# Reordering the first steps of a layernorm, attention and gated-FFN kernel

## The chip, the core and the metric

The kernel runs on one core of a Trainium2 chip. The core has five engines that each work through their own instructions in order: TensorE (PE in the profile: matmuls and transposes through the matrix array; PEld is its weight loads), VectorE (DVE), ScalarE (ACT), GpSimd (POOL) and SyncE (SP, which here only issues DMAs). They meet through semaphores. The metric is device time in microseconds (us), from start to end of the program. Lower is better.

## The reference, cut to what matters

Input x is 4 batches of 512 rows with 512 elements, in float32. All of it is computed:

```python
xn = layernorm(x)                                  # over the 512 elements, eps 1e-5
q = einsum("bpd,hde->bphe", xn, W_Q) + b_Q         # 16 heads of 128; k and v alike
s = where(causal, einsum("bqhe,bkhe->bhqk", q, k) / sqrt(128), -1e5)
z = einsum("bkhe,bhqk->bqhe", v, softmax(s))
attn = einsum("bqhe,hed->bqd", z, W_O) + b_O
f = (silu(xn @ gate_w.T * gate_s) * (xn @ up_w.T * up_s)) @ down_w.T * down_s
out = x + attn * silu(f)
```

The FFN's inner width is 1408. Its weights are -1, 0 or 1.

## The kernel before, in words

**Split numbers.** Matmuls run in a reduced float32 format. To keep precision, each operand is held as two parts: "hi" is the value rounded to that format (a cast, mostly on ScalarE), "lo" is what is left (a subtraction, on VectorE or GpSimd). A product is three matmuls: hi·hi, lo·hi and hi·lo. Two helpers issue them. `mm3` (lines 91 to 94) does one pair of operands in the order hi·lo, hi·hi, lo·hi. `mm3_all` (96 to 106) does a list of pairs: all hi·hi, then all lo·hi, then all hi·lo, and after each matmul it takes one step from the list `side`, if there is any. So steps put into `side` are woven between the matmuls of a projection.

**Order of work.** The whole program lies in a manual schedule: every engine runs its instructions in the order in which the Python code issues them. Nothing is planned by costs. Moving a line in the code moves its instructions in the queues of the engines that it uses.

**Buffers.** PSUM, where matmuls write, has two pools of tiles here: `ps_st` with three buffers (scores, even transposes) and `ps_mm` with five (projections `psq`, `psk`, `psv`, attention output `z`, output projection `pso`, odd transposes). A buffer can be written again when all readers of its former tile are done; for most tiles the last reader is the "lo" subtraction on VectorE.

**The start** (lines 517 to 569). Tiles of 128 rows of x are loaded. `ln_stats` does two VectorE instructions for each tile (statistics, aggregate), `ln_sd` a square root on ScalarE (which needs an activation table load), `ln_normalize` a reciprocal and a scaling on VectorE (tile `xn`). `ln_transpose` does four TensorE transposes per tile and the cast to hi on ScalarE (tile `xh`); `ln_low` is the lo part on VectorE (`xl`). Weights are loaded raw by `prepare`, which puts them on the list `pending` with a due number, and are split when `split_pending` is called with that number: a cast on ScalarE (line 150) and a subtraction (151) on GpSimd, or on the engine that is given. The first head's q and k are projected in halves, between the transposes of tiles 0, 1 and 2, 3.

**The heads** (581 to 681). 64 heads follow each other: eight groups of two attention heads, in each group four batches, in each batch two heads. The step of number n does, in this order: scores and softmax of head n (`softmax`: three score tiles on TensorE, four fused maximum steps on VectorE, four exponentials on ScalarE, four reciprocals on VectorE with a layernorm step of the list `between` after each if there is one, four scalings on GpSimd, line 342); for early heads the split of the former head's transposed p (`split_p`: cast at line 389 on ScalarE, subtraction at line 391 on VectorE, for early heads both halves there); the first projections of v (`fill`); the 32x32 transposes of p on VectorE (`turn_p`, 356), whose blocks a DMA round trip puts in place; weight splits that are due (`split_pending(n)`, line 617); loads; q and k projections of the next head; attention output z of the former head (`attend`, 423); and the rest of the v projections.

In steps 0, 2 and 4 (`ln_next`) the next batch's x is normalised too. Its statistics come a step before (`ln_b`, 644 and 658); in step 0 all four tiles come right before the projection of q. Its four `ln_normalize` steps stand in the list `norms`: in step 0 they run after q's projection (650), in steps 2 and 4 inside softmax. Its 16 transposes and four lows go into `side` and are woven into the last two v projections (662 to 668).

The output weights of group 0 (`wo0`, two tiles) are prepared in step 1 with due number 2, and first used by `pso` in step 3. The FFN (691 to 798) follows after all heads.

Of the kernel before, what the change touches and what calls it, by code (L numbers as in the profile page):

```python
# [43 lines left out]
def kernel(  # L44
# [46 lines left out]
    def mm3(ps, a, b, first, last):  # L91
        nc.tensor.matmul(ps, a.hi, b.lo, start=first, stop=False)  # L92
        nc.tensor.matmul(ps, a.hi, b.hi, start=False, stop=False)  # L93
        nc.tensor.matmul(ps, a.lo, b.hi, start=False, stop=last)  # L94

    def mm3_all(ps, pairs):

        todo = [
            (getattr(a, i), getattr(b, k))
            for i, k in (("hi", "hi"), ("lo", "hi"), ("hi", "lo"))  # L100
            for a, b in pairs
        ]
        for n, (l, r) in enumerate(todo):
            nc.tensor.matmul(ps, l, r, start=n == 0, stop=n == len(todo) - 1)  # L104
            if side:
                side.pop(0)()
# [5 lines left out]
    with ExitStack() as at:  # L112
# [15 lines left out]
        def load_x(b, t):  # L128
            xt = lnp.tile([P, D], F32, name="xt", tag="xt")
            nc.sync.dma_start(out=xt, in_=x[b, ts(t, P), :])  # L130
            x_in[b, t] = xt
# [5 lines left out]
        def load_const(src, shape, name):  # L137
            t = const.tile(shape, F32, name=name)
            nc.gpsimd.dma_start(out=t, in_=src)
            return t  # L140
# [5 lines left out]
            load_on[0].dma_start(out=r, in_=src)  # L146
            return r

        def split_w(dst, raw, on=nc.gpsimd):
            nc.scalar.copy(dst.hi, raw)  # L150
            on.tensor_tensor(dst.lo, raw, dst.hi32, ALU.subtract)

        def flat(s):
            return Split(s.hi.rearrange("p c e -> p (c e)"), s.lo.rearrange("p c e -> p (c e)"))
# [10 lines left out]

        def split_pending(n, on=nc.gpsimd):

            for due, dst, raw in [p for p in pending if p[0] <= n]:
                split_w(dst, raw, on)
            pending[:] = [p for p in pending if p[0] > n]  # L170

        def prepare(due, dst, src, name):

# [21 lines left out]

        mv_of, ln_of = {}, {}

        def ln_stats(b, tt):

            mv = small.tile([P, len(tt), 2], F32, name="mv")  # L200
            for k, t in enumerate(tt):
                st = small.tile([P, 6], F32, name="st")
                nc.vector.bn_stats(out=st, in_=x_in[b, t])
                nc.vector.bn_aggr(out=mv[:, k, :], in_=st)
            mv_of[b, tuple(tt)] = mv

        def ln_sd(b, tt):
            mv = mv_of.pop((b, tuple(tt)))
            sd = small.tile([P, len(tt)], F32, name="sd")
            nc.scalar.activation(sd, mv[:, :, 1], AF.Sqrt, bias=eps)  # L210
            for k, t in enumerate(tt):
                ln_of[b, t] = mv[:, k, :], sd[:, k : k + 1]
# [43 lines left out]
        def ln_low(b, t):  # L256
            lo_of.pop((b, t))()
# [38 lines left out]
        def softmax(qT, kT, between):  # L296
            p = pp.tile([P, NS * P], F32, name="p", tag="p")
            of = [p[:, row[t] : row[t] + (t + 1) * P] for t in range(NT)]
            nmax = {}
            for pack in PACK:  # L300
                sc = ps_st.tile([P, S], F32, name="sc", tag="st")
                at_ = 0
                where = {}
                for t in pack:
                    n = (t + 1) * P
                    where[t] = sc[:, at_ : at_ + n]
                    if t > 0:
                        mm3(where[t], qT[:, ts(t, P)], kT[:, :n], True, True)
                    at_ += n
                if 0 in pack:  # L310

                    two = sc[:, at_ - P : at_ + P]
                    nc.tensor.matmul(two, qT.hi[:, :P], kT.both[:, :, :P], start=True, stop=False)  # L313
                    nc.tensor.matmul(where[0], qT.lo[:, :P], kT.hi[:, :P], start=False, stop=True)
                for t in pack:
                    n = (t + 1) * P
                    add = mask[:, S - n :]
                    if t == 0:
                        add = small.tile([P, P], F32, name="add", bufs=1)
                        nc.vector.tensor_tensor(add, two[:, P:], mask[:, S - P :], ALU.add)  # L320
                    nmax[t] = small.tile([P, 1], F32, name="nmax", bufs=8)
                    nc.vector.tensor_tensor_reduce(  # L322
                        out=of[t],
                        in0=where[t],
                        in1=add,
                        scale=-SCALE,
                        scalar=BIG,
                        op0=ALU.add,
                        op1=ALU.min,
                        accum_out=nmax[t],  # L330
                    )
            for pack in PACK:
                for t in pack:
                    tot = small.tile([P, 1], F32, name="tot", bufs=8)
                    rtot = small.tile([P, 1], F32, name="rtot", bufs=8)
                    nc.scalar.activation(  # L336
                        of[t], of[t], AF.Exp, bias=nmax[t], scale=-1.0, accum_out=tot
                    )
                    nc.vector.reciprocal(rtot, tot)  # L339
                    if between:  # L340
                        between.pop(0)()
                    nc.gpsimd.tensor_scalar(of[t], of[t], rtot, 1.0, ALU.mult, ALU.mult)  # L342
            return of
# [34 lines left out]
        def split_p(raw, shared):  # L378
            pt = p_split()
            half = NQ // 2  # L380
            for k in range(0, NQ, half):
                src = raw[:, k : k + half].rearrange("p b (s i) -> p b s i", i=Q)

                def dst(part):
                    return part[:, :, k * Q : (k + half) * Q].rearrange(
                        "p s (b i) -> p b s i", i=Q
                    )

                nc.scalar.copy(dst(pt.hi), src)  # L389
                on = nc.gpsimd if shared and k == 0 else nc.vector  # L390
                on.tensor_tensor(dst(pt.lo), src, dst(pt.hi32), ALU.subtract)  # L391
            return pt
# [104 lines left out]
        def look():  # L497
            if looking:
                raw = looking.pop(0)
                nc.vector.tensor_tensor(bits, bits, raw.bitcast(I32), ALU.bitwise_or)  # L500
# [16 lines left out]
        with tc.manual_schedule():  # L517
# [22 lines left out]
            ln_transpose(0, 0)  # L540
            ln_transpose(0, 1)
            split_pending(-3)
            ln_stats(0, [2, 3])
            ln_low(0, 0)
            ln_low(0, 1)
            ln_sd(0, [2, 3])
            table(AF.Exp)
            ln_normalize(0, 2)
            ln_normalize(0, 3)
            split_pending(-2, nc.vector)  # L550
            prepare_qk(1, -1)
            q_of = project(0, 0, wq[0], bq_sb, "q", 2)
            k_of = project(0, 0, wk[0], bk_sb, "k", 2)
# [11 lines left out]
            split_pending(-1)  # L565
            for t in range(NT):
                load_x(1, t)
            bo_bc = load_const(b_o.broadcast_to([P, D]), [P, D], "bo_bc")
            ds_bc = load_const(down_s.broadcast_to([P, D]), [P, D], "ds_bc")

# [10 lines left out]
            for n, (g, b, i) in enumerate(heads):  # L581
# [12 lines left out]
                def fill(ks):  # L594
                    for t in ks:
                        if i == 0 and not (n == 0 and t == 0):
                            project_v(g, b, t)
                        if i == HG - 1 and prev is not None:
                            project_out(*prev, t, zs[prev])
# [7 lines left out]
                of = softmax(qT, kT, norms if n > 0 else [])  # L607
                if n > 1 and early:
                    pt = split_p(raw, B * HG < n < len(heads) - 2)
                look()  # L610
                half = NT // 2 if nxt is not None else NT - 1
                fill(range(0, half))
# [1 line left out]
                    raw_next = turn_p(of)  # L614
                if not early:
                    pt = split_p(raw, B * HG < n < len(heads) - 2)
                split_pending(n)

                if prev is not None:
                    cut = NT // 2 if n + HG < len(heads) else NT - 1  # L620
# [19 lines left out]
                if g > 0:  # L640
                    load_look()
                if nxt is not None:
                    if ln_b is not None and n != 1:
                        ln_stats(ln_b, range(NT))
                    nh = nxt[0] * HG + nxt[2]
                    *_, qT = project(nxt[1], nh, wq[nh], bq_sb, "q")
                    if n == 0:
                        ln_sd(ln_b, range(NT))
                        table(AF.Exp)
                    while norms:  # L650
                        norms.pop(0)()
# [7 lines left out]
                if ln_b is not None and n > 0:  # L659
                    ln_sd(ln_b, range(NT))  # L660
                    table(AF.Exp)
                if ln_next:
                    for t in range(NT):
                        side.extend(ln_transposes(b + 1, t))
                        side.append(lambda t=t: ln_low(b + 1, t))
                    fill(range(half, NT))
                    while side:
                        side.pop(0)()
                    if b + 2 < B:
                        for t in range(NT):  # L670
                            load_x(b + 2, t)
# [192 lines left out]
```

## Time and profile before

| | us |
|---|---|
| median of 3 runs | 1218.52 (1217.36 to 1219.19) |
| profiled execution | 1218.36 |
| its span, first to last instruction | 1217.0 |
| TensorE busy | 1199.1 |
| VectorE busy | 795.5 |
| ScalarE busy | 549.9 |
| GpSimd busy | 378.6 |
| mean granted TensorE clock | 0.997 of full |

In the lines of the profile, "L391" is line 391 of the kernel; "pt<-ptr,pt" names the tile written and the tiles read; "x2" counts instructions; brackets give the idle time of the engine just before, and what ended it. A line of waits gives the engine and line that waited, the engine and tile waited for, then the sum, the number and the longest in us. The share of busy time alone does not tell what a step costs: an engine may be late at one place and idle at another.

### The profile page before, as it was taken

How to read it: one execution, taken by the hardware profiler on the slowest of the kernel's cores; microseconds unless marked ns; L12 is line 12 of the kernel's file. 1: busy time of each engine (PE TensorE's matmuls, PEld its weight loads, DVE VectorE, ACT ScalarE, POOL GpSimd, SP SyncE). 2: the span in 40 equal slices, each digit the busy share in tenths (PEclk: the TensorE clock that was granted, in tenths of full speed). 3: DMA queues.
4: the chain of work that ended last, by engine and by line, in shares of the span. 5: the costliest groups of instructions: out<-in, count | busy, mean ns of one | idle time of the engine just before them, and what ended most of it. 6: DMA issues, size and time to landing. Idle time of an engine off the chain costs nothing.

```text
span 1217.0 us, 19221 instructions
## 1 busy us (share of the span) xinstructions
PE 1199.1 (99%) x6466; PEld 1047.4 (86%) x6466; DVE 795.5 (65%) x2149; ACT 549.9 (45%) x1272; POOL 378.6 (31%) x484
## 2 busy tenths in 40 slices
PE   7899999999999999999999999999999999999997
PEld 6788888888888888888888888888888888888886
DVE  6997767677777777776776676666667543433443
ACT  5654544454445545444544454545444332323231
POOL 3212332343234433432433252325231351202110
PEclk9999999999999999999999999999999999999999
DMA  5354456666665666666765655555555893727241
GB/s 168 111 177 156 150 174 194 200 193 196 191 208 173 194 206 213 191 199 203 210 184 173 186 182 172 186 179 173 175 166 166 270 306 87 216 79 217 77 147 38
DMA packets 117913, 215.55 MB, mean 177 GB/s; under 512 B 13232, under 2 KB 45744, under 8 KB 117808
## 3 DMA queue, kind: packets, MB, share of 16 engines
q1 hardware_dynamic: 74016, 134.51, 34.6%
q10 hardware_dynamic: 29376, 53.26, 14.4%
q0 software_dynamic: 14416, 26.48, 8.2%
q8 instruction: 53, 0.87, 0.3%
q14 instruction: 52, 0.43, 0.1%
HBM read 135.17 MB, written 79.04 MB: 176 GB/s over the span
## 4 chain that ended last, share of the span: by engine, by line
PE 96%; DVE 2%; ACT 0%; DMA 0%; issue 0%; SPq 0%; DVEq 0%; ACTq 0%
PE psv L104 15%; PE psq L104 14%; PE psk L104 14%; PE z L423 9%; PE pd L727 7%; PE pg L727 7%; PE pu L727 7%; PE pso L92 5%; PE pso L93 5%; PE pso L94 5%; PE sc L92 3%; PE sc L93 3%; PE sc L94 3%; PE sc L313 1%; PE tr L247 1%; PE z L426 1%
## 5 line engine op out<-in xcount | busy, mean ns | idle before, releaser
L342 POOL TENSOR_SCALAR p<-p,rtot 128x512 f32<-128x512 f32 (+3 forms) x256 | 148.6, 600 | 604.9 <-DVE rtot L339 580.3
L336 ACT ACTIVATE p<-p,nmax 128x512 f32<-128x512 f32 (+3 forms) x256 | 140.9, 553 | 111.6 <-DVE nmax L322 111.6
L356 DVE STREAM_TRANSPOSE sq<-p 128x256 f32<-128x256 f32 x378 | 113.2, 361 | 0.0
L279 ACT ACTIVATE q<-psq,consts 128x512 fp32r<-128x512 f32 (+1 forms) x65 | 44.4, 683 | 123.4 <-PE psq L104 50.3
L322 DVE CUSTOM_DVE_ANT_0 p<-sc,mask 128x512 f32<-128x512 f32 (+2 forms) x192 | 96.3, 551 | 1.3 <-PE sc L94 1.2
L280 DVE SCALAR_TENSOR_TENSOR k<-psk,consts,k 128x512 fp32r<-128x512 f32 (+1 forms) x65 | 48.1, 739 | 72.2 <-ACT k L279 72.2
L391 POOL TENSOR_TENSOR pt<-ptr,pt 128x640 fp32r<-128x640 f32 x53 | 83.7, 1580 | 8.8 <-ACT pt L389 8.4
L279 ACT ACTIVATE k<-psk,consts 128x512 fp32r<-128x512 f32 (+1 forms) x65 | 44.2, 680 | 90.4 <-PE psk L104 90.4
L389 ACT CAST pt<-ptr 128x640 fp32r<-128x640 f32 x126 | 85.0, 724 | 0.1
L280 DVE SCALAR_TENSOR_TENSOR q<-psq,consts,q 128x512 fp32r<-128x512 f32 (+1 forms) x65 | 47.9, 737 | 49.7 <-ACT q L279 48.1
L753 DVE SCALAR_TENSOR_TENSOR hd<-pu,consts,sg 128x512 f32<-128x512 f32 x44 | 33.0, 751 | 65.5 <-PE pu L727 61.0
L469 DVE TENSOR_TENSOR a<-pso,a 128x512 f32<-128x512 f32 x108 | 69.4, 682 | 0.3 <-issue 0.3
L391 DVE TENSOR_TENSOR pt<-ptr,pt 128x640 fp32r<-128x640 f32 x73 | 68.8, 953 | 1.1 <-ACT pt L389 1.1
L339 DVE RECIPROCAL rtot<-tot 128x1 f32<-128x1 f32 x256 | 41.6, 162 | 41.3 <-ACT p L336 35.1
L92 PE MATMUL sc<-k,q 128*128 128x512 f32 (+2 forms) x192 | 64.9, 338 | 1.1 <-DVE k L280 1.1
L93 PE MATMUL sc<-k,q 128*128 128x512 f32 (+2 forms) x192 | 64.7, 337 | 0.0
L94 PE MATMUL sc<-k,q 128*128 128x512 f32 (+2 forms) x192 | 64.7, 337 | 0.0
L423 PE MATMUL z<-pt,v_0h 128*128 128x512 f32 x128 | 50.7, 396 | 3.4 <-DVE pt L391 3.4
L336 ACT ACTIVATION_READ_ACCUMULATOR p<-p,nmax 128x1 f32 x256 | 47.7, 186 | 0.0
L423 PE MATMUL z<-pt,v_1h 128*128 128x384 f32 x128 | 44.2, 345 | 0.0
L783 ACT ACTIVATE o<-o 128x512 f32<-128x512 f32 (+1 forms) x17 | 10.3, 607 | 68.8 <-DVE o L782 68.8
L92 PEld LDWEIGHTS sc<-k,q 128*128 128x128 f32 x192 | 36.2, 188 | 5.3 <-DVE k L280 1.3
(762 smaller groups left out, 3418.3 us busy)
## 6 DMA issues: line engine op xcount, KB each, us to landing
turn<-sq SPq DMA_DIRECT2D x63, 640.0 KB, 3.4
ptr<-turn SPq DMA_DIRECT2D x252, 160.0 KB, 3.5
acc<-a SPq DMA_DIRECT2D x124, 256.0 KB, 3.3
a<-acc ACTq DMA_DIRECT2D x108, 256.0 KB, 3.0
xt<-in_x SPq DMA_DIRECT2D x16, 256.0 KB, 4.0
wor<-in_w_o ACTq DMA_DIRECT2D x16, 256.0 KB, 4.5
fa<-acc SPq DMA_DIRECT2D x16, 256.0 KB, 6.5
fx<-in_x SPq DMA_DIRECT2D x16, 256.0 KB, 6.9
```

Source lines behind the costliest of these rows:

```text
L92: nc.tensor.matmul(ps, a.hi, b.lo, start=first, stop=False)
L93: nc.tensor.matmul(ps, a.hi, b.hi, start=False, stop=False)
L94: nc.tensor.matmul(ps, a.lo, b.hi, start=False, stop=last)
L104: nc.tensor.matmul(ps, l, r, start=n == 0, stop=n == len(todo) - 1)
L280: nc.vector.scalar_tensor_tensor(q.lo[:, at_], ps, bias[:, h : h + 1], q.hi32[:, at_], ALU.add, ALU.subtract)
L322: nc.vector.tensor_tensor_reduce(out=of[t], in0=where[t], in1=add, scale=-SCALE, scalar=BIG, op0=ALU.add, op1=ALU.min, accum_out=nmax[t],)
L336: nc.scalar.activation(of[t], of[t], AF.Exp, bias=nmax[t], scale=-1.0, accum_out=tot)
L342: nc.gpsimd.tensor_scalar(of[t], of[t], rtot, 1.0, ALU.mult, ALU.mult)
L356: nc.vector.transpose(dst.rearrange("p a s i -> p s a i"), src.rearrange("p (s a i) -> p s a i", s=n, i=Q),)
L391: on.tensor_tensor(dst(pt.lo), src, dst(pt.hi32), ALU.subtract)
L423: nc.tensor.matmul(o, v, p_, start=k == 0, stop=k == len(todo) - 1)
L727: nc.tensor.matmul(ps, l, r, start=first and k == 0, stop=last and k == len(pairs) - 1)
```

## The change

- In the start, the statistics of tiles 2 and 3 are parted: those of tile 2, then the lows of tiles 0 and 1, then those of tile 3. `ln_stats` takes two more arguments for that. The casts of the first v weights move ahead of the square root of tiles 2 and 3; their subtractions stay where they were, on VectorE. `split_w` therefore gives the subtraction back as a function.
- The statistics of the first tile of batch 1 move from step 0's end to before step 0's softmax.
- In softmax the scores use `mm3_all` with one pair in place of `mm3`: hi·hi, lo·hi, hi·lo.
- In steps 2 and 4 two of the four normalisations stay in softmax, and two follow after it (in step 2 after the split of p).
- In step 2 (n equal to HG) the pending split, that of `wo0`, moves from before the q projection to after the last v projection.
- In steps 0, 2 and 4 eight empty steps stand ahead of the transposes in `side`, so that the transposes begin eight matmuls later, and the last ones follow after the projections.

```diff
-        def split_w(dst, raw, on=nc.gpsimd):
+        def split_w(dst, raw):
             nc.scalar.copy(dst.hi, raw)
-            on.tensor_tensor(dst.lo, raw, dst.hi32, ALU.subtract)
+            return lambda on: on.tensor_tensor(dst.lo, raw, dst.hi32, ALU.subtract)
...
         def split_pending(n, on=nc.gpsimd):
 
+            lows = []
             for due, dst, raw in [p for p in pending if p[0] <= n]:
-                split_w(dst, raw, on)
+                lows.append(split_w(dst, raw))
+                if on is not None:
+                    lows[-1](on)
             pending[:] = [p for p in pending if p[0] > n]
+            return lows
...
-        def ln_stats(b, tt):
-
-            mv = small.tile([P, len(tt), 2], F32, name="mv")
-            for k, t in enumerate(tt):
+        def ln_stats(b, tt, only=None, mv=None):
+
+            todo = list(enumerate(tt))
+            if only is not None:
+                todo = todo[:only] if mv is None else todo[only:]
+            if mv is None:
+                mv = small.tile([P, len(tt), 2], F32, name="mv")
+            for k, t in todo:
...
             mv_of[b, tuple(tt)] = mv
+            return mv
...
                     if t > 0:
-                        mm3(where[t], qT[:, ts(t, P)], kT[:, :n], True, True)
+                        mm3_all(where[t], [(qT[:, ts(t, P)], kT[:, :n])])
...
-                    if between:
+                    if len(between) > NT // 2:
                         between.pop(0)()
...
             split_pending(-3)
-            ln_stats(0, [2, 3])
+            wv_lows = split_pending(-2, None)
+            mv = ln_stats(0, [2, 3], 1)
             ln_low(0, 0)
             ln_low(0, 1)
+            ln_stats(0, [2, 3], 1, mv)
             ln_sd(0, [2, 3])
             table(AF.Exp)
             ln_normalize(0, 2)
             ln_normalize(0, 3)
-            split_pending(-2, nc.vector)
+            for low in wv_lows:
+                low(nc.vector)
...
             for t in range(NT):
                 load_x(1, t)
+            mv = ln_stats(1, range(NT), 1)
...
+                if n > 0:
+                    while norms:
+                        norms.pop(0)()
                 look()
...
-                split_pending(n)
+                if n != HG:
+                    split_pending(n)
...
-                    if ln_b is not None and n != 1:
+                    if n == 0:
+                        ln_stats(ln_b, range(NT), 1, mv)
+                    elif ln_b is not None and n != 1:
                         ln_stats(ln_b, range(NT))
...
                 if ln_next:
+                    side.extend([lambda: None] * (2 * ND))
                     for t in range(NT):
                         side.extend(ln_transposes(b + 1, t))
                         side.append(lambda t=t: ln_low(b + 1, t))
                     fill(range(half, NT))
+                    split_pending(n)
                     while side:
                         side.pop(0)()
```

## The prediction

> **What bounds the kernel now.** I read the page's busy times, then the waits of TensorE, then the order of time around each wait. First the page:
>
> ```profile
> PE 1199.1 (99%) x6466; PEld 1047.4 (86%) x6466; DVE 795.5 (65%) x2149; ACT 549.9 (45%) x1272; POOL 378.6 (31%) x484
> ```
>
> TensorE sets the time; an edit pays only if it removes TensorE idle time or slow clock. All its waits in the trace:
>
> ```profile
> PE z L423 <- DVE pt L391: 3.4, 1, 3.4
> PE tr L247 <- DVE xn L230: 2.2, 2, 2.0
> PE warm L222 <- POOL ident masks.py:199: 1.4, 1, 1.4
> PE psq L104 <- DVE xl L250: 1.3, 1, 1.3
> PE sc L92 <- DVE k L280: 1.1, 1, 1.1
> PE psq L104 <- ACT xh L249: 0.7, 1, 0.7
> ```
>
> All lie before 60 us; later TensorE is full, so what it is ahead after head 4 it keeps to the end. Around the second (head 0; columns: start, duration, engine):
>
> ```profile
> 28.60 0.18 DVE L204 BATCH_NORM_AGGREGATE mv<-st 128x2 f32<-128x6 f32 x1
> 28.70 0.72 DVE L280 SCALAR_TENSOR_TENSOR q<-psq,consts,q 128x512 fp32r<-128x512 f32 x1
> ...
> 29.52 0.55 DVE L230 TENSOR_SCALAR xn<-xt,mv,rstd 128x512 f32<-128x512 f32 x1
> ...
> 30.12 0.33 PE L247 MATMUL tr<-ident,xn 128*128 128x128 f32 x1 [2.01 <-DVE xn L230]
> ```
>
> Four statistics (from 25.53, 0.79 each) hold VectorE until 28.70; the transpose waits after one projection matmul. Around the first (head 2; the first line is the same work in head 1):
>
> ```profile
> 35.93 1.56 DVE L391 TENSOR_TENSOR pt<-ptr,pt 128x640 fp32r<-128x640 f32 x2
> ...
> 54.68 0.65 DVE L230 TENSOR_SCALAR xn<-xt,mv,rstd 128x512 f32<-128x512 f32 x1
> ...
> 55.16 3.10 POOL L151 TENSOR_TENSOR wo0l<-wor,wo0h 128x512 fp32r<-128x512 f32 x2
> 55.26 3.69 DVE L391 TENSOR_TENSOR pt<-ptr,pt 128x640 fp32r<-128x640 f32 x2
> ```
>
> The low part of p takes 3.69 us against 1.56, beside the split of wo on POOL. What the wait then does to the clock, in stretches (PEclk is the column after the busy times):
>
> ```profile
> 55.00:59.00 4.00, 0.63 (x5) 0.32 (x4) 4.00 (x4) 1.75 (x4) 3.16 (x3) 1.00 0.00 0
> 60.30:63.70 3.40, 3.40 (x18) 3.40 (x17) 3.40 (x8) 1.50 (x3) 0.00 (x0) 0.50 0.46 190
> ```
>
> Half clock for 3.4 us: from first transpose to scores is 6.09 us here (59.85 to 65.94), 4.58 in head 0 (30.12 to 34.70), so 1.5 lost.
>
> **What the Trainium skill says.** "GPSIMD Engine Reference", 8. Key points: GpSimd shares its SBUF interfaces with VectorE and collides with VectorE work that has two SBUF inputs. The trace agrees: 3.69 against 1.56. "TensorE: Matmul & The Clock Gate", What's actually happening: an idle window of about 3.4 us halves the clock, and a window's activity restores it. The trace agrees: 0.50 after 3.37 idle, none after 2.01. Same page, Architectural detail: VectorE and ScalarE are strict FIFOs, on which my running sums rest; every timeline here is in program order.
>
> **The change part by part**, by starting each instruction when its engine and its input are free, with this trace's durations.
>
> Start: VectorE does one statistic before the two lows instead of two. The lows end 0.80 earlier (8.45+1.26 = 9.7 against 10.53) and TensorE's 1.25 wait at 10.58 falls to 0.45. The price: the second statistic ends at 10.5, not 9.35, so xn of tile 3 is ready near 12.3 against 11.85, and TensorE, done with its projections at 11.8, waits some 0.1 between transposes. wv's casts move to 9.0–10.1 on ScalarE (its two loads land some 5.5 us after issue at 3.56), ahead of the sd at 10.5; its lows end at 13.5 against 13.04, needed at 13.7. I cost the cast move at nothing: ScalarE has a gap there. If the loads landed later than 9.5, each microsecond would delay sd, xn and the transposes by as much. Scores begin 0.6 earlier.
>
> Scores high first: 64 heads, 3 blocks. Only the first scores wait for k's low part (1.1). Two matmuls at 0.23 now pass before it is needed: 0.5 gained once, nothing elsewhere; each matmul loads its weights in either order. Pack two starts near 18.7 (19.83): 1.1 ahead.
>
> Head 0: one statistic (0.79) goes to 18.4–19.1, into VectorE's idle 1.17 before 20.15; the scores arrive near 19.0, so it costs 0.1. Its input is among loads issued from 10.34, 4.0 to landing. The softmax is about 0.8 ahead (POOL's two issues, 0.72+0.56, and p's scaling shift by 0.6), its 32x32 transposes end at 24.7 (25.53), three statistics at 27.1 (28.70), and the first xn, 1.42 later, at 28.5. TensorE issues psv from 26.7, and eight empty steps let nine matmuls (1.1) pass before the transpose at 27.8: wait 0.7 for 2.0. The rest of the block is eight matmuls shorter (4.58-0.92): head 1's scores at 32.2 for 34.70, 2.5 ahead.
>
> Head 1: VectorE is full from 28.70 to 39.5; it leaves 1.75 ahead (starts 1.6 ahead, lows reordered), so k's low part is ready at 41.9 (43.63). TensorE arrives at 41.3 and has 0.46 of high work: 0.2 wait. Its scores of head 2 end 2.4 ahead. z ends near 41.3, z0 and four statistics follow on VectorE 2.57 ahead, so do the square root, table and exps of head 2.
>
> Head 2: p's low part no longer waits for two norms (1.7) nor beside wo. It starts at 53.67-2.57 = 51.1. POOL still scales two tiles there (0.86), which stretches 1.47 to some 2.05: ready 53.15. TensorE's z starts at 51.67, its third group at 53.07: wait 0.1 for 3.37. z ends 53.85 for 59.73: 5.9 ahead. Without the idle window no half clock: 1.5 more.
>
> Given back: the two norms (1.30) and v0's low (0.34) now stand before psv's buffer comes free. Five PSUM buffers go round, psv2 takes psv0's: free at 54.8, wait 1.0. The odd transpose takes psq's, free when q's low ends (57.5; TensorE 56.95): 0.6. This reuse isn't in the trace; if other buffers are free it is 0, if both add in full 1.6; I take 1.6. Scores of head 3 start at 60.1 (65.94), 5.8 ahead.
>
> wo's split moves behind psv3 (end 59.75): v3's cast to 60.5, wo's two casts to 61.05 and 61.6 (1.14), POOL's two lows, 1.30 each, to 62.4 and 63.7. No DMA moves: both loads were issued at 39.5, and buffers of the next loads are others. Queued behind: xh of tile 3 (61.6–62.2), then its low and head 3's first maximum on VectorE at 62.9 (67.11), 4.2 ahead. TensorE ends scores at 61.85, waits 0.6 for the first half of wo, does 0.7, waits 0.6 for the second. If POOL ran at its slow 1.55 this is 1.7, if head 3's scores wait for buffers instead, 0; I take 1.2. Head 4's projection starts at 65.85 for 70.50: 4.65 ahead.
>
> The other edits at nothing: in heads 2 and 4 the empty steps only reorder the same matmuls (transposes then follow two projections, where xn is long ready; without that cover it would be 0.66 per norm), and head 4's two late norms (1.3) trade places with POOL contention of the same row (four norms there take 3.9, with 2.6 alone).
>
> Later: head 4's k low is ready at 75.8, scores due at 76.0; head 4's p low at 87.4, due 87.4. So VectorE no longer costs TensorE more than 0.1, and from 92.9 it has idle time.
>
> Sum: 1.1 + 1.4 - 0.1 + 3.5 - 1.6 + 1.5 - 1.2 = 4.6 (at each step: 1.1, 2.5, 2.4, 5.9, 5.8 with both of the next terms, 4.65). The profiled execution took 1218.36 (span 1217.0), so 1213.7; the median, 1218.52, lies 0.16 above it: 1213.9. The bounds above move it by 1.6 and 1.2 one way, 0.5 the other.
>
> **Rivals.** Nothing new waits: buffers are free and wo's lows find cover. For it: PSUM reuse isn't visible. Against: VectorE has no gap in head 2. Gain 4.6+1.6+1.2 = 7.4 at most; beyond 5.8 gained, time 1211.1–1212.7.
>
> The given-back waits are larger: wo's lows at 1.84 (the longest seen), p's low at 3.0 rather than 2.05, and TensorE idles until both. Against: nothing beside wo now has two SBUF inputs. Gain 2.4–3.5: 1215–1216.1.
>
> The change doesn't do what it says: VectorE's total work sets TensorE's place after head 2 whatever the order. For it: VectorE is 9.0 of 10 busy from 20 to 100. Against: POOL contention alone wasted 2.1 of its time and it stood idle for 1.17 and 1.10. Within 2.4: 1217.5.
>
> Slower: the new scores order makes consecutive matmuls change their stationary operand; before, the first two of three share q's high part. If a change costs c, 192 blocks cost 192c; it decides above (4.6+2.4)/192 = 36 ns. Against: starts at 43.88, 44.12, 44.35 and 44.59 are 0.24, 0.23, 0.24 apart, with and without a change. At 40 ns: 1213.9+7.7 = 1221.6.
>
> **How the numbers follow.** Gain 3.5–5.8: 0.50, own range 1212.7–1215.0; no new wait 0.21; larger waits 0.14; no change 0.09; slower 0.06. Faster 0.85 (the first three), same 0.09, slower 0.06; a measurement of this kernel tells about 0.2% (2.4 us) from no change. Range 1211.5–1216.5: it leaves out some 0.07 below and 0.13 above.
>
> **What would show it.** Right: first scores near 18, first transpose of head 0's second batch waiting 0.7, no half clock near 60 us, L391 of head 2 near 2 us, z waiting under 0.5, new waits of psv and tr in head 2 (for v's and q's low) and of pso for wo's low on POOL. Wrong: a wait over 3.4 us anywhere before 100 us (half clock again), p's low of head 2 still above 3 us, TensorE waits after 100 us, or score matmuls more than 0.24 us apart.

## The result and the profile after

| | before | after |
|---|---|---|
| median of 6 runs each, us | 1219.09 (1217.36 to 1219.81) | 1213.24 (1212.62 to 1215.02) |
| profiled execution, us | 1218.36 | 1212.96 |
| its span, us | 1217.0 | 1211.2 |
| mean granted TensorE clock | 0.997 | 0.999 |

The ratio of the times is 0.9955, with a 95% interval of 0.9943 to 0.9968: 0.45% faster, 5.85 us by the medians. The forecast was 1213.9 us, a gain of 4.6. Run again later, the changed kernel came out at 0.9956 (0.9943 to 0.9970).

The page's busy times after the change:

```profile
PE 1198.4 (99%) x6466; PEld 1045.7 (86%) x6466; DVE 792.5 (65%) x2149; ACT 549.3 (45%) x1272; POOL 379.1 (31%) x484
```

TensorE does the same 6466 matmuls in 0.7 us less busy time, while the span is 5.8 us shorter. So most of the gain must be idle time that is gone. It shows in the waits of TensorE:

```profile
PE warm L231 <- POOL ident masks.py:199: 1.4, 1, 1.4
PE pso L92 <- POOL wo0l L151: 0.7, 2, 0.4
PE psq L104 <- ACT xh L258: 0.7, 1, 0.7
PE psv L104 <- DVE v_0l L275: 0.6, 1, 0.6
PE sc L104 <- ACT k L288: 0.6, 1, 0.6
PE tr L256 <- DVE xn L239: 0.5, 1, 0.5
PE tr L256 <- DVE q L289: 0.3, 1, 0.3
```

The wait of z for p's low part (3.4) and that of the first projection for xl (1.3) are gone, the wait of the first transpose for xn fell from 2.0 to 0.5, and the scores wait for k's high part (0.6) and no longer for its low part (1.1). Three kinds of wait are new, those of pso (two), of psv and of the transpose for q's low part. Head 0, in order of time (start, duration, engine, line):

```profile
26.23 0.18 DVE L212 BATCH_NORM_AGGREGATE mv<-st 128x2 f32<-128x6 f32 x1
...
27.15 0.55 DVE L239 TENSOR_SCALAR xn<-xt,mv,rstd 128x512 f32<-128x512 f32 x1
...
27.75 0.33 PE L256 MATMUL tr<-ident,xn 128*128 128x128 f32 x1 [0.50 <-DVE xn L239]
```

The statistics end at 26.41 (28.78 before), and the transpose starts at 27.75 (30.12). Head 2:

```profile
50.34 1.53 DVE L400 TENSOR_TENSOR pt<-ptr,pt 128x640 fp32r<-128x640 f32 x2
50.45 2.32 POOL L351 TENSOR_SCALAR p<-p,rtot 128x256 f32<-128x256 f32 x2 [0.44 <-DVE rtot L348]
51.98 0.55 DVE L239 TENSOR_SCALAR xn<-xt,mv,rstd 128x512 f32<-128x512 f32 x1
...
53.57 0.73 PE L104 MATMUL psv<-wv0h,xh 128*128 128x256 f32 x4 [0.60 <-DVE v_0l L275]
...
59.81 2.54 POOL L151 TENSOR_TENSOR wo0l<-wor,wo0h 128x512 fp32r<-128x512 f32 x2 [7.05 <-ACT wo0h L150]
...
61.16 0.50 PE L92 MATMUL pso<-wo0l,z0h 128*128 128x512 f32 x1 [0.41 <-POOL wo0l L151]
```

p's low part takes 1.53 in place of 3.69. Beside it, it is POOL that is slow: its two scalings (line 351) take 2.32, or 1.69 and 0.65 one by one, where the same two took 0.48 and 0.38 before. wo's split now runs beside head 3's scores, 9.5 us after the start of p's low part. In stretches of 3.4 us (PEclk is the number after the busy times) the clock stays whole where it was halved:

```profile
56.80:60.20 3.40, 3.40 (x28) 3.27 (x27) 3.19 (x7) 2.44 (x6) 0.39 (x1) 1.00 0.47 176
60.20:63.60 3.40, 2.71 (x14) 1.91 (x13) 2.70 (x11) 1.98 (x7) 2.15 (x2) 1.00 1.06 248
```

**A correction for comparing single traces.** The third tile of x arrived at 7.64 us in the trace of before and at 6.90 in that of after (start of its statistic). Over the fourteen traces of this study it arrived between 6.73 and 7.76, in no order that follows the edits, so 0.74 us of the difference between those two traces is chance. Below, a place in a trace is given "after arrival", that is, less this start. TensorE's place at the start of head 8's q projection, where it has been full for 50 us, is then 131.45 - 7.64 = 123.81 before and 125.52 - 6.90 = 118.62 after: **a gain of 5.19**. The rest of the difference of the profiled executions (5.40) is the 0.74 of the arrival, less 0.40 of time outside the span (1.36 before, 1.76 after; more on this under the eight empty steps), less 0.13 that is lost after head 8.

### The profile page after: what moved, and what is told of

Same layout as the page of the kernel before. It is cut to its first block, busy times and chain, and to the rows that moved or that the text cites. A ratio compares the mean times of both kernels' runs of the same rounds, so it can differ in the third digit from the quotient of the medians.

```text
span 1211.2 us, 19214 instructions
## 1 busy us (share of the span) xinstructions
PE 1198.4 (99%) x6466; PEld 1045.7 (86%) x6466; DVE 792.5 (65%) x2149; ACT 549.3 (45%) x1272; POOL 379.1 (31%) x484
## 4 chain that ended last, share of the span: by engine, by line
PE 94%; issue 2%; DVE 2%; DMA 1%; POOL 1%; ACT 0%; SPq 0%; ACTq 0%; POOLq 0%; DVEq 0%
PE psv L104 14%; PE psq L104 14%; PE psk L104 13%; PE z L432 8%; PE sc L104 8%; PE pd L748 7%; PE pg L748 7%; PE pu L748 7%; PE pso L92 5%; PE pso L93 5%; PE pso L94 5%; PE sc L322 1%; PE z L435 1%; DMA wqr<-in_w_q 1%; DVE sq L365 0%
## 5 line engine op out<-in xcount | busy, mean ns | idle before, releaser
L104 PE MATMUL sc<-k,q 128*128 128x512 f32 (+2 forms) x576 | 111.8, 338 | 0.6 <-ACT k L288 0.6
L104 PEld LDWEIGHTS sc<-k,q 128*128 128x128 f32 x576 | 98.9, 188 | 11.4 <-ACT k L288 0.8
L772 ACT ACTIVATE sg<-pg,consts 128x512 f32<-128x512 f32 x44 | 30.3, 688 | 17.4 <-PE pg L748 17.4
L432 PE MATMUL z<-pt,v_2h 128*128 128x256 f32 x128 | 35.9, 280 | 0.0
```

The lines of the kernel that those rows point to most:

```text
L432: nc.tensor.matmul(o, v, p_, start=k == 0, stop=k == len(todo) - 1)
```

## The experiments

The kernels were timed in groups, and each group had its own runs of the kernel before; that is why its median is a range in the table. My theory is the sum in the prediction: waits at separate places, each with its price. The rivals that the runs were to tell apart were that VectorE's total work decides whatever the order; that one of the two large moves does everything; that the new order of the scores has a price in every head; and, for what exceeded the forecast, chance.

| kernel | median, us | ratio to before (95%) | head 8 after arrival |
|---|---|---|---|
| before | 1218.17 to 1219.09 | 1 | 123.81 |
| changed kernel | 1213.24 | 0.9955 (0.9943 to 0.9968) | 118.62 |
| changed kernel again | 1213.25 | 0.9956 (0.9943 to 0.9970) | 118.65 |
| norms back | 1213.82 | 0.9962 (0.9948 to 0.9975) | 118.96 |
| wo's split back | 1214.27 | 0.9965 (0.9952 to 0.9979) | 119.30 |
| both back | 1216.67 | 0.9982 (0.9972 to 0.9992) | 122.45 |
| before, with only these two moved | 1215.77 | 0.9978 (0.9970 to 0.9987) | 121.00 |
| before, TensorE kept busy in z's wait | 1218.17 | 1.0000 (0.9992 to 1.0008) | 122.93 |
| start back | 1214.35 | 0.9963 (0.9949 to 0.9976) | 119.27 |
| statistic back | 1214.53 | 0.9961 (0.9948 to 0.9975) | 119.46 |
| no empty steps | 1212.99 | 0.9953 (0.9939 to 0.9966) | 119.36 |
| old order of scores | 1213.49 | 0.9964 (0.9950 to 0.9977) | 118.91 |
| late norms later still | 1212.40 | 0.9954 (0.9941 to 0.9968) | 117.41 |
| the same, wo's split back | 1211.80 | 0.9948 (0.9934 to 0.9962) | 117.27 |

The times alone tell only the large differences apart: an interval is some 1.5 us to each side. The small ones rest on the traces.

### Head 2: norms and wo's split, each undone

Norms back: all four normalisations in softmax again, also in step 4.

```diff
-                    if len(between) > NT // 2:
+                    if between:
                         between.pop(0)()
...
-                if n > 0:
-                    while norms:
-                        norms.pop(0)()
                 look()
```

> The changed kernel with one part undone: all four normalisations of heads 2 and 4 stand in softmax again; wo's split stays at its new place. My theory (p's low part was late for two reasons, norms ahead of it and GpSimd beside it): p's low in head 2 starts some 1.7 us later, still takes near 1.5, TensorE's third group of z waits about 1.5, v0's low then follows at once, so that the wait of psv falls away. No half clock. Net 0.3 to 1.3 us slower than the changed kernel. Rival 'the norms' order is all': the whole gain in head 2 goes, 2.7 us or more slower, half clock back.

p's low part starts 1.56 later (52.48 - 7.48 = 45.00 after arrival, for 50.34 - 6.90 = 43.44), and it takes 1.54: wo isn't beside it. Its line, and TensorE's line of waits, which says what that costs:

```profile
52.48 1.54 DVE L400 TENSOR_TENSOR pt<-ptr,pt 128x640 fp32r<-128x640 f32 x2
...
PE z L432 <- DVE pt L400: 1.2, 1, 1.2
```

1.2 us of idle time leave the clock whole, and the waits of psv (0.6) and of the odd transpose (0.3) are gone in return. Head 8 is 0.34 later than in the changed kernel. This speaks against the rival that the norms' order is everything.

wo's split back at its old place:

```diff
-                if n != HG:
-                    split_pending(n)
+                split_pending(n)
...
                     fill(range(half, NT))
-                    split_pending(n)
                     while side:
```

> The changed kernel with one part undone: wo's split stands ahead of the q projection in step 2 again; the norms stay at their new places. My theory: p's low part is done near 51.8 before wo's lows start on GpSimd (near 51.7), so it stays near 1.5 us; the two late norms run beside GpSimd and grow from 0.55 to about 1.0 each, psv's wait for v0's low grows by some 0.8, and the waits for wo's low (0.7) go. Net within 0.7 us of the changed kernel. Rival 'the place of wo is what counts': p's low takes above 3 us again, z waits over 2 us, 3 us or more slower.

Now POOL's split meets the second late normalisation instead of p's low part:

```profile
52.75 0.55 DVE L239 TENSOR_SCALAR xn<-xt,mv,rstd 128x512 f32<-128x512 f32 x1
...
53.40 1.65 DVE L239 TENSOR_SCALAR xn<-xt,mv,rstd 128x512 f32<-128x512 f32 x1
...
53.51 2.68 POOL L151 TENSOR_TENSOR wo0l<-wor,wo0h 128x512 fp32r<-128x512 f32 x2
...
55.44 0.74 PE L104 MATMUL psv<-wv0h,xh 128*128 128x256 f32 x4 [1.66 <-DVE v_0l L275]
```

The second normalisation takes 1.65 for 0.55, and v's low part, which stands behind it, comes 1.1 later: psv waits 1.66 for 0.60. The two waits of pso are gone, and this makes up for it: head 4's projection starts 57.58 after arrival, 57.67 in the changed kernel. Yet at head 8 TensorE is 0.68 later. This is lost in head 4, where VectorE is still 1.1 late (k's low part ends 68.27 after arrival for 67.20): the scores start before k's low part is done, and the third group of z waits for p's low part:

```profile
PE z L432 <- DVE pt L400: 0.2, 1, 0.2
```

Both back:

> The changed kernel with norms and wo's split of head 2 as before; all else changed. My theory: p's low takes 3.7 us again, z waits about 3.3 us for it (TensorE and VectorE both came some 3.2 us earlier to head 2), the half clock may follow; about 2.7 us slower than the changed kernel, so some 3 us faster than before. Rival 'VectorE's total work sets TensorE's place after head 2 whatever the order': no slower than the changed kernel.

Its edit is the two above together. In order of time:

```profile
51.96 3.08 POOL L151 TENSOR_TENSOR wo0l<-wor,wo0h 128x512 fp32r<-128x512 f32 x2
52.03 3.69 DVE L400 TENSOR_TENSOR pt<-ptr,pt 128x640 fp32r<-128x640 f32 x2
...
55.77 0.79 PE L432 MATMUL z<-pt,v_0h 128*128 128x512 f32 x1 [3.32 <-DVE pt L400]
```

In stretches (the first is taken inside the wait):

```profile
54.00:55.70 1.70, 0.00 (x0) 0.00 (x0) 1.70 (x2) 0.00 (x0) 1.04 (x1) 0.76 0.00 0
56.80:60.20 3.40, 3.40 (x17) 3.40 (x17) 3.25 (x8) 0.69 (x1) 0.00 (x0) 0.50 0.37 155
60.20:63.60 3.40, 3.40 (x25) 3.40 (x25) 1.68 (x3) 1.68 (x4) 0.00 (x0) 0.78 0.55 147
```

The old picture is back, 3.69 and all, and worse: with a wait of 3.32 the clock is halved for about twice as long. The mean of 0.76 between 54.00 and 55.70 says that it fell near 54.9, while TensorE still waits, and the 0.78 of the last stretch that it was back near 61.7: some 6.8 us. In the kernel before it fell at 60.3, after TensorE had taken up work again at 58.99, and stayed for 3.4. From the end of the wait to head 3's scores it is 7.99 us here, 5.50 with only the norms back (the same work at full clock): 2.5 lost, where before lost 1.6 (6.95 against 5.37 in the filled kernel below) after a wait of 3.37. Head 8 is 3.83 later than in the changed kernel (forecast 2.7), and by the ratios the time is 0.0026 of 1218.4, 3.2 us, longer. VectorE does the same work in all four kernels, so the rival "VectorE's total work decides" falls.

The two moves are substitutes: undoing one costs 0.34 or 0.68, undoing both 3.83. Either one alone parts p's low part from wo's split, so that TensorE's longest wait in head 2 is 1.2 or 1.66 in place of 3.32, and the clock stays whole.

### The two moves alone, on the kernel before

The two edits above in the other direction, and nothing else.

> The kernel before with only the norms and wo's split moved. My theory: z's wait of 3.4 us and the half clock go, new waits of psv (0.6) and of pso for wo (0.7) come; 3.8 us (3 to 4.5) faster than before, so this pair is the larger part of the change. Rival 'total work': no more than 1 us faster.

The gain is 2.81 by the trace and 2.6 by the medians (1215.77 against 1218.39). This missed the expectation of 3.8 (3 to 4.5). z's wait and the half clock are gone, and head 3's scores start 4.2 earlier (after arrival), near what was expected, but head 4's projection only 2.8 earlier. Between them:

```profile
63.68 0.50 PE L92 MATMUL pso<-wo0l,z0h 128*128 128x512 f32 x1 [0.46 <-POOL wo0l L151]
...
64.92 0.50 PE L92 MATMUL pso<-wo0l,z1h 128*128 128x512 f32 x1 [0.28 <-POOL wo0l L151]
```

The two waits add up to 0.74, but from head 3's scores to head 4's projection it is 5.94 against 4.56 before, 1.38 more. A wait costs more than the idle time that its line gives: consecutive matmuls overlap (this one lasts 0.50 and the next starts 0.33 later, while in a full stretch they last 0.40 and start 0.23 apart), and after a wait that overlap is lost. In the changed kernel the same two waits list 0.69 and the same block takes 5.82, 1.26 more than before. So a listed wait of TensorE stands here for roughly 0.2 to 0.3 more than its figure.

### TensorE kept busy during the wait, on the kernel before

24 transposes of the identity stand in TensorE's queue ahead of the z matmuls that waited, in step 2. VectorE's and POOL's work is untouched.

```diff
             for k, (o, v, p_) in enumerate(todo):
+                if fill_at and k == fill_at:
+                    warm_up(FILLER)
...
```

`FILLER` is 24, and `fill_at` is set for the z of step 2 alone.

> The kernel before with 24 idle transposes (of the identity, into a tile that nobody reads) in TensorE's queue ahead of the third group of z in step 2, where it waits 3.4 us for p's low part. It takes away TensorE's idleness, not its lateness. My theory: the half clock of 3.4 us is the price of an idle stretch of about that length, so it goes; head 3's scores start 1.5 us earlier (64.4 for 65.94), 1.5 us faster than before. Rival 'the clock falls for another reason (load, chance)': still half clock, no faster.

The transposes fill the wait but for 0.8, and the clock stays at 1.00 in every stretch. Waits, filler and the stretch that was slow before:

```profile
PE sc L93 <- DVE k L281: 1.4, 2, 1.1
...
PE z L426 <- DVE pt L392: 0.8, 1, 0.8
```

```profile
55.20 2.78 PE L223 MATMUL warm<-ident 128*128 128x128 f32 x24
...
58.76 0.50 PE L426 MATMUL z<-pt,v_0h 128*128 128x512 f32 x1 [0.77 <-DVE pt L392]
```

```profile
60.20:63.60 3.40, 3.40 (x32) 3.40 (x31) 3.40 (x9) 2.22 (x5) 0.00 (x0) 1.00 0.48 198
```

Head 3's scores come 1.57 earlier, the 1.5 that I put on the half clock. But head 4's scores wait 0.3 for k's low part, a wait that before didn't have: VectorE is no earlier, so TensorE gives part of its lead back. 0.88 is left at head 8 in these traces. In the times nothing is left (1218.17 both; the interval is 1 us to each side), so this missed the expectation on time. The single traces overstate it: the profiled execution of the filled kernel (1217.06) was the second fastest of its 13. The clock isn't the reason: the mean granted clock was 0.996 or 0.997 in all 17 executions of the kernel before in this group, and 0.998 or 0.999 in 11 of the 13 of the filled one. Why a higher clock gains nothing in the median stays open.

### The parts before head 2, each undone

Start back: the statistics of tiles 2 and 3 together before the lows of tiles 0 and 1, wv's casts after the square root.

```diff
-            wv_lows = split_pending(-2, None)
-            mv = ln_stats(0, [2, 3], 1)
+            ln_stats(0, [2, 3])
             ln_low(0, 0)
             ln_low(0, 1)
-            ln_stats(0, [2, 3], 1, mv)
...
-            for low in wv_lows:
-                low(nc.vector)
+            split_pending(-2, nc.vector)
```

> The changed kernel with the start as before (both statistics ahead of the two lows, casts of the v weights after the square root). My theory: the wait of psq for the lows comes back (near 1.2), head 0's scores start 0.6 later, counted from the arrival of the third x tile, and all later stages with them: 0.6 us slower (0.3 to 0.8). Rival 'hidden': the wait for xn in head 0 shrinks by as much, no slower.

Head 8 is 0.65 later, as expected. The listed wait for the lows of tiles 0 and 1 came back at only 0.5, where 1.2 was expected. The trace has one wait more that no other has, 0.64 of a psv for q's low part at 474 us; it lies far behind the edit, and it isn't in the 0.65.

Statistic back: all four statistics of the next batch in step 0 together, before the q projection.

```diff
-            mv = ln_stats(1, range(NT), 1)
...
-                    if n == 0:
-                        ln_stats(ln_b, range(NT), 1, mv)
-                    elif ln_b is not None and n != 1:
+                    if ln_b is not None and n != 1:
                         ln_stats(ln_b, range(NT))
```

> The changed kernel with all four statistics of batch 1 at their old place. My theory: the first transpose of head 0 waits 1.2 to 1.3 for 0.5, heads 1 and 2 are 0.8 later: 0.8 us slower (0.5 to 0.9). Rival 'hidden': head 2's scores were due when k's low part was, so no more than 0.3 slower.

Head 8 is 0.84 later: one statistic takes 0.79 there. The first transpose waits 1.3 for 0.5 (the other wait in this line, 0.5, is at 6 us, in the start):

```profile
PE tr L256 <- DVE xn L239: 1.8, 2, 1.3
```

No empty steps:

```diff
-                    side.extend([lambda: None] * (2 * ND))
```

> The changed kernel without the eight empty steps. My theory: head 0's first transpose waits 1.5 for 0.5, since only one matmul goes ahead of it, head 1's scores start 0.95 later; in head 2 the odd transpose's wait (0.3) goes; 0.65 us slower in all (0.4 to 1.0). Rival 'VectorE sets head 2': TensorE's loss in head 0 is taken up in head 1, no slower.

By the trace head 8 is 0.74 later (0.65 expected); the transposes wait again, before any projection that could cover them (1.5 in head 0; the rest of the line is in the start):

```profile
PE tr L256 <- DVE xn L239: 2.4, 2, 1.5
```

But the time isn't longer (1212.99, against 1213.25 in the same group). In part this lies outside the span: execution less span is 1.3 to 1.5 us in all timed runs of the kernels without the empty steps (this one, before and the two made from it), but 1.7 to 1.9 in all those of the kernels that have them. By the profiled executions it is 1.39 here and 1.76 in the changed kernel. So the empty steps cost 0.4 us there, and the rest of the 0.74 is within the intervals. What it is that takes this 0.4 the runs don't show.

Old order of the scores: `mm3` in softmax.

```diff
-                        mm3_all(where[t], [(qT[:, ts(t, P)], kT[:, :n])])
+                        mm3(where[t], qT[:, ts(t, P)], kT[:, :n], True, True)
```

> The changed kernel with the scores in the old order (hi.lo first). My theory: the first scores start some 0.45 us later and head 2's wait 0.4 for k's low; 0.5 us slower in all, starts of score matmuls 0.23 to 0.24 apart as in the changed kernel. Rival 'the order of the stationary operands has a price over 64 heads': the time differs by more than 2 us, or the spacing differs by 10 ns or more.

Head 8 is 0.29 later, where 0.5 was expected: the wait for k's low part is 1.1 again at head 0, and part of the loss is taken up later. The heads after that change nothing (0.31 at the end of the trace), so the rival in which the new order has a price per head falls with its 7.7 us.

The changed kernel again:

> The changed kernel once more, as the measure for the three runs beside it and for one question: in its profile the third tile of x came 0.74 us earlier than in the profile of the kernel before. My theory: that is chance of the loads and no effect of the change; the arrival lies anywhere between 6.8 and 7.8 us, and head 4's projection starts 57.7 us after that statistic begins, within 0.2, whatever the arrival. Rival 'the change brings the loads earlier': it arrives near 6.9 again.

Head 4's projection starts 57.66 us after arrival (57.67 in the first trace) and the time is 1213.25 (1213.24). The arrival happened to be early again (6.74), so this run alone says little about the correction. The kernels that are the same as the changed one up to head 0's scores say more (norms, wo's split or both back, statistic back, no empty steps, the two of the next part). With the changed kernel's own two they are nine traces: the arrival lies anywhere from 6.73 to 7.67 in them, and head 0's scores are done between 12.16 and 12.29 after it. So the arrival is chance, and TensorE's place follows it.

The single undoings add up to 0.65 + 0.84 + 0.74 + 0.29 + 3.83 = 6.35 us, more than the 5.19 gained together. A likely reason, not tested by itself, is that each was taken out of a kernel in which the others had already made TensorE early, so that lateness of VectorE is felt at once.

### Past the change: the late norms later still

The new waits of psv and of the odd transpose (for v's and q's low parts) stand behind the two late norms. Without the new loop these run after the q projection, where the old loop already stands:

```diff
-                if n > 0:
-                    while norms:
-                        norms.pop(0)()
                 look()
```

> The changed kernel with the two late norms of heads 2 and 4 still later, after the q projection, behind v's lows, p's 32x32 transposes and q's low. My theory (psv and the odd transpose wait because the norms hold back the VectorE reads that free their PSUM buffers): both waits (0.6 and 0.3) go, 0.9 us faster than the changed kernel at head 3's scores. Rival 'VectorE's total work': head 3 starts no earlier.

Both waits are gone, and so are those of pso; a wait of head 3's scores for the last xl is new:

```profile
PE sc L104 <- DVE xl L259: 0.4, 1, 0.4
```

Head 8 is 1.21 earlier (0.9 was expected at head 3's scores, where it is 1.28). This is what reuse of PSUM buffers would do: the edit changes no operand of psv, only when the low parts that read the older tiles are done.

With this, wo's split was put back at its old place too, by the edit shown above:

> As the run before, and wo's split back at its old place, where VectorE now runs instructions that read PSUM or one SBUF tile beside it. My theory (only VectorE work with two SBUF inputs[...] collides with GpSimd): no instruction grows, the waits of pso for wo's low (0.4 and 0.3) go too, and the cast of tile 3 comes 1.1 earlier; 1.6 us faster than the changed kernel. Rival 'anything beside GpSimd slows': no gain, VectorE's transposes or lows take above 1.5 times their time.

```profile
52.78 2.54 POOL L151 TENSOR_TENSOR wo0l<-wor,wo0h 128x512 fp32r<-128x512 f32 x2
52.79 1.79 DVE L365 STREAM_TRANSPOSE sq<-p 128x256 f32<-128x256 f32 x6
54.52 0.70 DVE L289 SCALAR_TENSOR_TENSOR q<-psq,consts,q 128x512 fp32r<-128x512 f32 x1
```

wo's split runs at its full speed (2.54) beside VectorE's 32x32 transposes and q's low part, and these take what they take elsewhere (q's low part 0.70, mean of its line 0.74). The place is harmless once no normalisation and no low part of p is beside it. But it gains next to nothing: head 8 is 1.35 earlier than in the changed kernel, 0.14 more than with the late norms alone, where 1.6 was expected. The waits of pso, which this edit was to remove, had already gone with the late norms. Of all kernels here this one has the lowest times, 1211.51 to 1211.82, all below those of the changed kernel (1212.62 and up), though not in the same group of runs; the ratios' intervals overlap.

## Why the prediction was right

The gain was 5.19 after arrival, or 5.85 by the medians, against 4.6. By its steps, places taken after arrival:

| step | forecast lead | measured |
|---|---|---|
| head 0's scores done (start, statistic, scores' order) | 1.1 | 20.89 - 19.07 - 0.74 = 1.08 |
| head 1's scores begin | 2.5 | 34.70 - 31.28 - 0.74 = 2.68 |
| head 2's scores done | 2.4 | 45.65 - 42.50 - 0.74 = 2.41 |
| z done | 5.9 | 59.90 - 52.97 - 0.74 = 6.19 |
| head 3's scores begin | 5.8 | 65.94 - 58.75 - 0.74 = 6.45 |
| head 4's projection | 4.65 | 70.50 - 64.57 - 0.74 = 5.19 |
| head 8's projection | the same | 5.19 |

- **What bounds it.** Right: all of the gain is made before 65 us and none is added or lost from head 4 to head 8.
- **Start, statistic, empty steps, scores' order.** Right in size (forecast 2.5 together at head 1's scores, measured 2.68). The transpose waits 0.50 for the 0.7 forecast. The wait of the first q projection for the lows, forecast at 0.45, didn't appear: at an arrival of 6.90 the lows come that much earlier. In two runs with the same start and an arrival like that of before (7.66 and 7.67) it is 0.54 and 0.56.
- **Head 2.** Right in mechanism: p's low part apart from wo's split, no idle window, no half clock. The step that failed is the size of p's low part: "POOL still scales two tiles there, which stretches 1.47 to some 2.05". It took 1.53. The Trainium skill ("GPSIMD Engine Reference", 8. Key points) says that the two engines share their SBUF interfaces and collide; I took it that VectorE is the one held. Here POOL was: 2.32 for two scalings, 0.86 before. The traces show why: p's low part started first (50.34, the scaling at 50.45), while in the kernel before POOL's subtraction did (55.16, p's low part at 55.26); more on this at the end. VectorE was therefore free 0.5 earlier, and the waits behind it came out smaller: psv 0.60 for 1.0, the transpose 0.32 for 0.6. The lead at head 3's scores exceeded the forecast by 0.65; 0.29 of this was there when z was done, and the rest came with these smaller waits.
- **Reuse of PSUM buffers.** Right in mechanism, though it had no line in the trace of before: the waits appeared at psv and at the odd transpose for the tiles named, and went with the late norms. Their size was 0.92 for the 1.6 put on them.
- **wo's split.** 1.2 forecast, 6.45 - 5.19 = 1.26 measured, but not as worked out: the two waits list 0.41 and 0.28, not 0.6 each; the rest is the overlap of matmuls that a wait breaks, which the sum had not counted. So the agreement of 1.2 with 1.26 is luck. The two moves were also credited with 3.5 together, when either one has nearly all of it.
- **Half clock.** 1.5 was put on it, and 1.57 came back in the filled kernel. That this lead would also stay to the end holds only when VectorE is earlier too, as it is in the changed kernel; alone, 0.88 stayed in the trace and nothing in the times. So the size of this term rests on single traces. The Trainium skill ("TensorE: Matmul & The Clock Gate", What's actually happening) says that an idle window of about 3.4 us halves the clock, and the traces agree in size: waits of 1.2 and 2.0 leave the clock at 1.00, waits of 3.32 and 3.37 halve it. But TensorE need not idle for a whole 3.4 us first: with both moves back the clock fell some 2.4 us into the wait of 3.32. The 3.4 us that the prediction named as a sign of a new half clock was therefore too high. How long the clock then stays halved differed too, 3.4 us in one and some 6.8 in the other.

Of the rivals, "nothing new waits" would have gained 7.4 and fell with the three new waits; the larger waits, the total work and the price per head fell as shown.

## What to carry to other kernels

Where two engines slow each other, find the pair of operations that collides ahead of a TensorE wait and part it by the cheaper of the two moves; the second move then earns little. If they must meet, let the instruction that TensorE waits for start first. Beware of waits of TensorE of 3 us and more: 3.3 us halved the clock here and 2.0 did not, and nothing between was tried. Count on recovered TensorE time only as far as the engines that feed it are earlier too. Before single traces are compared, take off the arrival of the first loads, and add some 0.2 to 0.3 us to each listed wait of TensorE for the overlap that it breaks.

## What the hardware showed that I had not expected

- Where VectorE and POOL collide they take turns, and the one that starts first, while the other is free, keeps its own time. Read one by one, in the kernel before: POOL's subtraction starts at 55.16 and takes 1.30, its own time. The first half of p's low part starts at 55.26 and ends 0.68 after it, so it takes 1.88 for 0.80. POOL's second subtraction ends 1.12 after that, and the second half of p's low part again 0.68 after that. After the change p's low part starts first: its halves take 0.80 and 0.81, and POOL's scaling ends 0.26 after the second, so it takes 1.69 for 0.48.
- So the same pair can go either way. A normalisation, which reads one large tile, and POOL's last scaling start together before (54.68), and VectorE is slow: 0.65 for 0.55, with POOL at its own time:

```profile
54.68 0.38 POOL L342 TENSOR_SCALAR p<-p,rtot 128x128 f32<-128x128 f32 x1 [0.44 <-DVE rstd L228]
```

- After the change the normalisation starts first (51.98, the scaling at 52.11), and POOL is slow: 0.65 for 0.38, with VectorE at 0.55. Who comes next when one already waits isn't settled by the order of start. With wo's split back, the normalisation of 53.40 waits for POOL's scaling, but wo's subtraction, which starts 0.10 after it, goes ahead (1.65 for 0.55); before, the waiting half of p's low part went ahead of POOL's second subtraction.
- wo's subtraction on POOL beside 32x32 transposes and a low part that reads PSUM slowed neither. (Spans on POOL are rough in this profile; those of VectorE, and what waits for it, carry the reading.)
- Nearly equal idle times of 3.37 and 3.32 us were followed by about 3.4 and 6.8 us of half clock, a loss of 1.6 and of 2.5 us.
- Arrival of the third input tile varied by 1.0 us from execution to execution (6.73 to 7.76), and the time outside the span differed by 0.4 us between kernels with and without eight empty steps in the order of issue, in every run.
